# A planned four-layer graph kernel: a weight product by seven half-size products, a turned product as a 64x64 burst, and new ranks for the last pairs of groups

## The chip, the cores and the metric

The kernel runs on one core of a Trainium2 chip. That core has a matrix engine (TensorE, PE in the profile) with its own queue of weight loads (PEld), a vector engine (VectorE, DVE), a scalar engine (ScalarE, ACT), a general engine (GpSimd, POOL) and a queue that issues DMAs (SyncE, SP). Each engine works through its own list of instructions in order and waits on semaphores for the others. Products land in PSUM[...]; everything else is held in SBUF. The metric is the device time of one execution in microseconds (us).

## The reference

The input x has 128 graphs of 64 nodes with 256 features, all in fp32, and one 64 x 64 matrix `adj` is shared by all graphs. Four layers follow each other, and each ends in `x = layernorm(x + layer(x))`:

```python
# layer 0: three times a weight and the squared adjacency
h = relu(adj*adj @ (x @ W1)); h = relu(adj*adj @ (h @ W2)); y = adj*adj @ (h @ W3)
# layer 1: U holds the eigenvectors of the normalised Laplacian of adj
h = relu((U.T @ x) @ W1 + b1); y = U @ (h @ W2 + b2)
# layer 2: two graph convolutions, then LSTMs over windows of p = 1, 2, 3, 4 nodes
h = relu(adj @ (x @ Wg0 + bg0)); h = relu(adj @ (h @ Wg1 + bg1))
for p in (1, 2, 3, 4): h[:, last node of each window] = lstm_last(Wih[p-1], Whh[p-1], ..., windows of h)
# layer 3: attention over the graph
h = x @ W + b_lin; y = softmax(where(h @ h.T * adj == 0, -1e16, h @ h.T * adj)) @ h + b
```

The products of one graph with `adj`, `U` or their transposes are over 64 nodes. Two graphs fill the 128 partitions, so these products are made with 64 x 64 blocks.

## The kernel before

The 8192 rows (128 graphs x 64 nodes) are cut into 64 row tiles of 128 rows. Four row tiles are a group, and there are 16 groups.

Layer 0 and the eigenvectors come first, in an order written by hand (`layer0`, `eigen`); the change doesn't touch them. They end at about 830 us of the profile.

After that, layers 1 to 3 are not emitted in the order of the source. A planner (`Plan`) takes notes of all operations, and `Plan.run` simulates the engines with assumed costs and emits, again and again, the operation that can start first. Its rules, as far as the change and the prediction need them:

- A unit of work is a pair of groups (`unit`): layer 1 (`layer1`) and the first part of layer 2 (`to_lstm`) for each group, then the LSTMs of window 3 and 4 for both together (`long`), then the rest of layer 2 (`from_lstm`) and layer 3 (`layer3`) for each. There are eight pairs, and at most four (`UNITS`) are in flight. A new one begins when one has ended. So the list of pairs that are still to begin (`todo`) is empty once the fourth pair has ended.
- Of the operations of one engine that can start within 0.02 us of the first, the one with the lowest `rank` is taken. The rank is `op.due`, which is the group's number times `PERIOD` (17.0) less the operation's `tail`, the time of the longest chain of operations behind it in its unit. When at most `LASTS` (2) groups are left, PE prefers the group with the most operations left.
- Tiles are taken from a fixed number of slots for each kind: eight PSUM banks (`ps`), `WIDE` = 9 tiles of 1024 columns (`w`, asked for with `work()`), `NARROW` = 3 of 512 columns (`v`, asked for with `work2()`). An operation that needs a tile can't start before a slot is free.
- `products` and `run` note matmuls with 0.00167 us per column and at least 0.223 us each; a burst of 32 matmuls of 64 x 64 (`mixed`) is noted with `QUADS` = 1.17 us.

In the profile all these operations have line L162, the line of `emit`; so they are told apart by tiles and shapes.

In `layer1` (one call for each group) the rows are multiplied with the eigenvectors by a burst (`mixed(xs, u2)`), then with `bw1`, two row tiles at a time; bias and relu follow, and the result `h` is multiplied with `ut2`, a 128 x 128 matrix with the 64 x 64 eigenvector matrix twice on its diagonal and zeros elsewhere:

```python
products([(pz[:, i, :], h[:, i, :], ut2, True, True) for i in (t, t + 1)])
```

These four matmuls turn h and multiply it at the same time. ACT copies their bank to the tile `z`, which is the stationary operand of the next product.

In `to_lstm` the second weight of layer 2 (`cw1`, 256 x 256) is multiplied with the mixed rows `a` (256 x 512), half of the output at a time (`c`), in two matmuls of 512 columns into one bank each. DVE then scales, adds a bias (`scalar_tensor_tensor`) and ACT applies the relu and writes `hT`, in which nodes and graphs are exchanged.

Elsewhere the kernel already multiplies 2 x 2 blocks with seven products of blocks in place of eight (Winograd's form of Strassen's method): in layer 0 (`seven` there is a local function of the layer-0 part) and in the LSTM gates (`fast`, with sums of weights from `add_weights`). In these forms the first product stays in its PSUM bank and later ones are added to it; the bank is read several times on the way, so the products of one such chain alternate with the reads.

Of the kernel before, what the change touches and what calls it, by code (L numbers as in the profile page):

```python
# [11 lines left out]
F32 = mybir.dt.float32  # L12
AF = mybir.ActivationFunctionType
ALU = mybir.AluOpType
# [89 lines left out]
class Plan:  # L104
# [59 lines left out]
    def run(self, units, ways):  # L164
# [4 lines left out]
        def rank(op):  # L169
            if op.engine == "PE" and not todo and len(left) <= LASTS:  # L170
                return -left[op.group]
            return op.due

        def candidates(guard):
            oldest = min([u for u in going if u] or [0])
# [581 lines left out]
EPS = 1e-5  # L757
UNITS = 4
ENDING = (14, 15)
WIDE = 9  # L760
NARROW = 3
GATES = 6
ATT = 2
CELLS = 2
OUTS = 2
LASTS = 2
PERIOD = 17.0
FARS = 8

RING = 4  # L770
# [59 lines left out]
def kernel(  # L830
# [138 lines left out]
    def run(out, pairs):  # L969
        for i, (lhsT, rhs) in enumerate(pairs):  # L970
            mm(out, lhsT, rhs, i == 0, i == len(pairs) - 1)
# [85 lines left out]
    def seven(n, product, c11, c12, c21, c22, last):  # L1057

        def view(b):
            return b[:, :2 * n].rearrange("p (i n) -> p i n", i=2)  # L1060

        def add(dst, b):
            VL.tensor_add(dst, dst, b)
            if last is relu:
                relu(dst, dst)

        ch = view(bank("ch"))
        product(ch, 1, True)
        step(lambda: S.copy(c11, ch))
        yield  # L1070
        b2 = view(bank())
        product(b2, 2, True)
        step(lambda: add(c11, b2))
        yield
        product(ch, 6, False)
        step(lambda: S.copy(c12, ch))  # L1076
        yield
        b5 = view(bank("b5"))
        product(b5, 5, True)
        step(lambda: S.copy(c22, b5))  # L1080
        yield
        product(ch, 7, False)
        step(lambda: add(c22, ch))
        yield
        product(b5, 3, False)
        step(lambda: add(c12, b5))
        yield
        product(ch, 4, False)
        step(lambda: last(c21, ch))
        yield  # L1090
# [164 lines left out]
    def add_weights(p, ready):  # L1255
        ways[p] = []
        names = "igo" if p == 1 else "ifgo"
        for k, w in enumerate((wih[p - 1], whh[p - 1])):
            if w is None:
                continue  # L1260
            nq = len(names)
            s = wb.tile([P, 3, nq, P], F32, name=f"sums{p}{k}")
            if p == 4:
                spare[0] = lambda s=s: s[:, 0, 0:2, :].rearrange("p q n -> p (q n)")
            s, w = plan.tile("sums", [P, 3, nq, P], s), plan.tile("sums", [P, 2, nq * 2 * P], w)
            a11, a12, a21, a22 = whole = quarters(w)
            S1, S2, S4 = (s[:, j] for j in range(3))
            V.tensor_add(S1, a21, a22, ready=ready)
            V.tensor_sub(S2, S1, a11, ready=ready)
            V.tensor_sub(S4, a12, S2, ready=ready)  # L1270
            V.tensor_sub(a21, a11, a21, ready=ready)
            raw = [{q: x[:, i] for i, q in enumerate(names)} for x in whole]
            sums = [{q: s[:, j, i] for i, q in enumerate(names)} for j in range(3)]
            ways[p].append([raw[0], raw[1], raw[3], *sums[:2], raw[2], sums[2]])

    def products(calls, also=(), **kw):

        size = lambda x: x.at.size if isinstance(x, Part) else int(np.prod(x.shape[1:]))
        cost = sum(max(0.001673 * size(c[2]) + 0.003, 0.223) for c in calls)
        plan.note("PE", [("matmul", (o, l, r), {"start": a, "stop": z, **kw}) for o, l, r, a, z in calls], cost,  # L1280
                  also=also)
# [11 lines left out]
    def work2():  # L1293
        return plan.tile("v", [P, 512])

    def ps4(shape=(P, 512)):
        return plan.tile("ps", shape)

    def as3(t, a):
        return t.rearrange("p (a b) -> p a b", a=a)  # L1300

    def relu(dst, src):
        S.activation(dst, src, AF.Relu)

    def mixed(src, rhs):

        dst = as3(work(), 2)
        to = dst.rearrange("p c (t h n) -> p h c t n", h=2, n=N)
        ps = [ps4((P, 2, 4, N)) for _ in range(2)]
        plan.note("PE", [("matmul", (ps[h][m, c, t, :], src[hs, t, f], rhs[hs, hs]), {"start": True, "stop": True})  # L1310
                         for t in range(4) for c in range(2) for m, f, h, hs in quads(c)], QUADS)
        V.tensor_copy(to[:, 0], ps[0])
        S.copy(to[:, 1], ps[1])
        return dst
# [22 lines left out]
    def layer1(xs):  # L1337
        a = mixed(xs, u2)
        for t in range(0, 4, 2):
            V.tensor_add(xs[:, t:t + 2, :], xs[:, t:t + 2, :], ub2.unsqueeze(1).to_broadcast([P, 2, D]))  # L1340
        h = as3(work2(), 4)
        z = work2()
        pz = ps4((P, 4, P))
        for t in range(0, 4, 2):
            p = ps4((P, 2, P))
            for j in range(2):
                run(p[:, j, :], [(a[:, k, (t + j) * P:(t + j + 1) * P], bw1[:, k, :]) for k in range(2)])
            V.tensor_add(h[:, t:t + 2, :], p, wide["b_b1"].unsqueeze(1).to_broadcast([P, 2, P]))
            relu(h[:, t:t + 2, :], h[:, t:t + 2, :])
            products([(pz[:, i, :], h[:, i, :], ut2, True, True) for i in (t, t + 1)])  # L1350
        S.copy(as3(z, 4), pz)
        for t in range(0, 4, 2):
            p = ps4((P, 2, D))
            for j in range(2):
                run(p[:, j, :], [(z[:, (t + j) * P:(t + j + 1) * P], bw2)])
            V.tensor_add(xs[:, t:t + 2, :], p, xs[:, t:t + 2, :])
            norm(xs[:, t:t + 2, :], False, twice=True)

    def to_lstm(xs, there):
        a = mixed(xs, adH2)  # L1360
        Q.dma_start(there, xs, cost=0.35)
        g1 = as3(work(), 4)
        for t in range(0, 4, 2):
            p = ps4((P, 2, D))
            for j in range(2):
                run(p[:, j, :], [(a[:, k, (t + j) * P:(t + j + 1) * P], cw0[:, k, :]) for k in range(2)])
            V.tensor_add(g1[:, t:t + 2, :], p, wide["c_b0"].unsqueeze(1).to_broadcast([P, 2, D]))
            relu(g1[:, t:t + 2, :], g1[:, t:t + 2, :])
        a = mixed(g1, adT2)
        hT = plan.tile("w", [P, 1024]).rearrange("p (k n b) -> p k n b", k=2, b=8)  # L1370
        for c in range(2):
            p = ps4((P, 4, P))
            run(p, [(cw1[:, k, c * P:(c + 1) * P], a[:, k, :]) for k in range(2)])
            h = work2()
            V.scalar_tensor_tensor(as3(h, 4), rs_row.unsqueeze(1).to_broadcast([P, 4, P]), cb1[:, c:c + 1], p,
                                   op0=ALU.mult, op1=ALU.add, cost=0.666)
            S.activation(hT[:, c, :, :].rearrange("p n b -> p b n"), as3(h, 8), AF.Relu, scale=2.0, cost=0.933)
        singles(hT)
        pairs(hT)
        return hT  # L1380
# [272 lines left out]
    def unit(groups):  # L1653

        if groups[0] == 0:
            add_weights(1, 10.0)
            add_weights(2, 30.0)
            add_weights(3, 45.0)
            add_weights(4, 60.0)
        there, hTs = [], []  # L1660
        for g in groups:
            plan.group = g + 1
            x = plan.tile("rows", [P, 4, D])
            there.append(plan.tile("rest", [P, 4, D], rest[g]))
            if g < RING:
                x.tile.real, x.tile.slot, x.tile.unit = rows_of(g), g, plan.unit
                plan.slots["rows"][g] = 1e9
                for i, op in enumerate(reversed(plan.pieces)):
                    if g == RING - 1 - i // 14:
                        half = np.arange(4 * D) // (2 * D) == i // 7 % 2  # L1670
                        x.tile.past.append((op, True, (0, P), half))
            else:
                Q.dma_start(x, there[-1], cost=0.35)
            layer1(x)
            hTs.append(to_lstm(x, there[-1]))
        plan.group = groups[0] + 1
        for p in (3, 4):
            long(hTs, p)
        late = plan.late
        for g, r, hT in zip(groups, there, hTs):  # L1680
            plan.group = g + 1
            x = plan.tile("rows", [P, 4, D])
            Q.dma_start(x, r, cost=0.35, after=late)
            from_lstm(x, hT, g)
            if g in ENDING:
                layer3(x, g, 0, 2)
                layer3(x, g, 2, 2)
            else:
                layer3(x, g, 0, 4)
# [56 lines left out]
```

## Time and profile before

| | us |
|---|---|
| three runs | 2305.53, 2307.65, 2307.74 |
| median | 2307.65 |
| the profiled execution | 2305.56 |
| its span, first to last instruction | 2303.8 |
| first of layer 1's bursts (`ps<-u,X`) | 832.8 |
| last product with the second weight of layer 2 (`ps<-w,cw`) | 2122.4 |
| last store of the fourth pair of groups, and of the seventh | 1882.0, 2227.3 |
| last store of all | 2301.2 |

PE is the engine that hardly rests. The busy time of each engine in four windows of the planned part, in us:

| window | PE | DVE | ACT |
|---|---|---|---|
| 1000 to 1050 | 50.0 | 26.7 | 25.7 |
| 1450 to 1500 | 47.8 | 43.8 | 30.4 |
| 2100 to 2150 | 48.9 | 45.2 | 31.6 |
| 2250 to 2300 | 34.2 | 27.4 | 25.1 |

How to read it: each matmul's modelled end overlaps the start of the next, so the sum of their durations is more than the engine's time; the distance from one start to the next is what a matmul costs in a full queue. A fp32 matmul is two records. In a timeline the columns are start, length, engine, line, operation, output and inputs, shapes and count; the bracket at the end of a line tells how long the engine had been idle and what it waited for.

### The profile page before, as it was taken

The numbers are of one execution on the slowest core, as the hardware profiler recorded it, in microseconds if no ns is written. First come the engines' busy times: TensorE is split into PE (matmuls) and PEld (weight loads), VectorE is DVE, ScalarE is ACT, GpSimd is POOL, SyncE is SP. The second block draws the span as 40 slices with busy tenths as digits, with TensorE's granted clock in tenths as the row PEclk, the third lists the DMA queues.
The fourth block names the chain that finished last, engine by engine and source line by source line (L and its number), as shares of the span: only waits on it lengthen the run. The fifth ranks groups of instructions, "written<-read, shape, count | busy, mean of one in ns | idle before, by whom it ended". The sixth has DMA issues, their size and how long they took to land.

```text
span 2303.8 us, 51099 instructions
## 1 busy us (share of the span) xinstructions
PE 2250.2 (98%) x20132; PEld 1985.7 (86%) x20132; DVE 1730.2 (75%) x5704; ACT 1196.0 (52%) x2892; POOL 137.0 (6%) x315
## 2 busy tenths in 40 slices
PE   8999999999999989999999999999999999999996
PEld 6788888878888778999989999899899899998895
DVE  5887877777888878666857967867866876878764
ACT  3444444443444336655556655555555655655654
POOL 0000000000000010000100100100000000000001
PEclk9999999999999999999999999999999999999998
DMA  7000000000000040000201211221211211312300
GB/s 242 11 11 11 10 11 11 19 11 11 11 10 2 1 161 20 19 1 27 85 22 57 75 56 40 78 72 40 77 56 49 76 65 31 104 58 93 99 19 19
DMA packets 80113, 107.87 MB, mean 47 GB/s; under 512 B 23296, under 2 KB 64256, under 8 KB 79872
## 3 DMA queue, kind: packets, MB, share of 16 engines
q1 hardware_dynamic: 79520, 104.32, 14.1%
q8 instruction: 158, 2.59, 0.5%
q14 instruction: 83, 0.68, 0.1%
q10 hardware_dynamic: 352, 0.28, 0.0%
HBM read 57.64 MB, written 45.09 MB: 45 GB/s over the span
## 4 chain that ended last, share of the span: by engine, by line
PE 86%; DVE 9%; ACT 1%; DMA 1%; issue 1%; POOL 1%; SPq 1%; DVEq 0%; ACTq 0%; POOLq 0%
PE ps L162 53%; PE ch L965 14%; PE ps L965 9%; PE b L965 6%; PE ps L1030 2%; DVE w L162 1%; DVE X L162 1%; DVE gates L162 1%; DVE st L162 1%; POOL rs L162 1%; DMA w<-far 1%; ACT gates L162 1%; PE pa L312 1%; SPq L162 1%; DVE D L52 1%
## 5 line engine op out<-in xcount | busy, mean ns | idle before, releaser
L162 PE MATMUL ps<-w,wih 128*128 128x128 f32 (+2 forms) x2944 | 573.0, 298 | 5.1 <-DVE gates L162 4.2
L162 PEld LDWEIGHTS ps<-w,wih 128*128 128x128 f32 x2944 | 454.3, 191 | 40.0 <-issue 13.5
L162 PE MATMUL ps<-w,sums 128*128 128x128 f32 (+2 forms) x3104 | 476.8, 294 | 5.7 <-DVE w L162 5.1
L162 PEld LDWEIGHTS ps<-w,sums 128*128 128x128 f32 x3104 | 419.9, 191 | 23.4 <-DVE w L162 6.4
L162 ACT ACTIVATE gates<-gates,cbi 128x256 f32<-128x256 f32 (+4 forms) x736 | 314.5, 479 | 189.0 <-DVE gates L162 186.0
L162 DVE TENSOR_TENSOR gates<-gates,ps 128x512 f32<-128x512 f32 (+4 forms) x408 | 235.9, 583 | 191.6 <-PE ps L162 182.4
L162 ACT COPY gates<-ps 128x512 f32<-128x512 f32 (+4 forms) x408 | 205.0, 507 | 238.1 <-PE ps L162 232.7
L162 PE MATMUL ps<-hs,whh 128*128 128x128 f32 (+1 forms) x896 | 182.2, 285 | 2.3 <-DVE hs L162 2.3
L162 PE MATMUL ps<-w,whh 128*128 128x128 f32 (+1 forms) x896 | 181.1, 284 | 0.0
L162 PEld LDWEIGHTS ps<-hs,whh 128*128 128x128 f32 x896 | 140.6, 193 | 2.5 <-DVE hs L162 2.5
L162 ACT ACTIVATE gates<-ps,cbi 128x128 f32<-128x128 f32 (+2 forms) x368 | 119.3, 385 | 42.2 <-PE ps L162 41.0
L162 PEld LDWEIGHTS ps<-w,whh 128*128 128x128 f32 x896 | 139.7, 191 | 0.0
L974 ACT ACTIVATE h<-h 128x512 f32<-128x512 f32 x96 | 60.5, 630 | 150.2 <-DVE h L52 150.2
L965 PE MATMUL ch<-m,tw 128*128 128x256 f32 x512 | 124.9, 382 | 3.0 <-ACT h L1076 1.7
L965 PE MATMUL b<-ss,aw 128*128 128x256 f32 x512 | 121.9, 379 | 0.0
L965 PE MATMUL ps<-aw,m 128*128 128x512 f32 x256 | 116.2, 606 | 1.2 <-ACT m L1036 1.2
L965 PEld LDWEIGHTS ch<-m,tw 128*128 128x128 f32 x512 | 94.7, 190 | 19.1 <-DVE h L52 3.7
L965 PEld LDWEIGHTS b<-ss,aw 128*128 128x128 f32 x512 | 96.8, 190 | 12.9
L162 POOL TENSOR_SCALAR rs<-mv 128x2 f32<-128x2 f32 x96 | 25.3, 272 | 1353.1 <-DVE mv L162 1351.7
L965 PEld LDWEIGHTS ps<-aw,m 128*128 128x128 f32 x256 | 48.3, 194 | 55.5 <-issue 51.5
L162 PE MATMUL ps<-hs,sums 128*128 128x128 f32 (+1 forms) x448 | 90.6, 284 | 0.0
L1036 ACT COPY m<-ps 128x512 f32<-128x512 f32 x96 | 51.2, 587 | 75.5 <-PE ps L1030 75.0
(360 smaller groups left out, 4077.4 us busy)
## 6 DMA issues: line engine op xcount, KB each, us to landing
far<-w SPq DMA_DIRECT2D x42, 512.0 KB, 2.7
w<-far SPq DMA_DIRECT2D x168, 128.0 KB, 3.2
X<-rest SPq DMA_DIRECT2D x24, 512.0 KB, 3.4
out_dram<-X SPq DMA_DIRECT2D x64, 128.0 KB, 1.7
rest<-XA SPq DMA_DIRECT2D x12, 512.0 KB, 2.6
rest<-X SPq DMA_DIRECT2D x12, 512.0 KB, 2.7
XA<-in_x_dram SPq DMA_DIRECT2D x22, 256.0 KB, 6.0
aw<-in_a_w_dram SPq DMA_DIRECT2D x3, 1024.0 KB, 10.2
```

Of the source, the lines that this page charges most:

```text
L52: return getattr(self.engine, name)(out, *args, **kw)
L162: getattr(e, name)(*[real(x) for x in args], **{k: real(v) for k, v in kw.items()})
L312: PE.matmul(out, lhsT, rhs, start=True, stop=True)
L965: PE.matmul(out, lhsT, rhs, start=start, stop=stop, **kw)
L974: S.activation(dst, src, AF.Relu)
L1030: PE.matmul(p[h][m, k, t, :], src[hs, t, f], sqT2[hs, hs], start=True, stop=True)
L1036: S.copy(to[:, h, c:c + 2], p[h])
```

## The change

Six edits, all outside layer 0:

1. In `to_lstm` the product with `cw1` is made of seven products of 128 x 128 weight blocks with 256 columns of `a`, in place of eight in two banks. DVE makes the sums of blocks of `a` (`sums_moving`) and adds the products up (`take`, `add`); the sums of weight blocks are made once (`sums_of`).
2. In `layer1` the product with `ut2` is made of 16 matmuls of 64 x 64 after all of `h` is there; its result lies in two banks, of which DVE copies one and ACT the other.
3. Once no pair is left to begin, the rank is the group's number times `LATE` (9.0) less the tail.
4. `WIDE` is 10 and `NARROW` 5.
5. The space kept for DMA descriptors is set to 1024 bytes.
6. `sums_of("cw1", ...)` is called at the start of the first pair.

```diff
@@ Plan.run
-            return op.due
+            return op.due if todo else op.group * LATE - op.tail
@@ constants
-WIDE = 9
-NARROW = 3
+WIDE = 10
+NARROW = 5
+LATE = 9.0
@@ new functions
+    def sums_of(key, w, stationary, ready):
+        s = plan.tile("sums", [P, 3, P], wb.tile([P, 3, P], F32, name=f"sums_{key}"))
+        (w00, w01), (w10, w11) = two_by_two(plan.tile("sums", [P, 2, D], w))
+        t1, t2, t4 = (s[:, i] for i in range(3))
+        if stationary:
+            V.tensor_add(t1, w01, w11, ready=ready)
+            V.tensor_sub(t2, t1, w00, ready=ready)
+            V.tensor_sub(t4, w10, t2, ready=ready)
+            V.tensor_sub(w01, w00, w01, ready=ready)
+            sevens[key] = [None, w00, w10, t4, w11, t1, t2, w01]
...
+    def sums_moving(b, spare):
+        (b00, b01), (b10, b11) = b
+        t1, t2 = spare
+        V.tensor_sub(t1, b01, b00)
+        V.tensor_sub(t2, b11, t1)
+        V.tensor_sub(b01, b11, b01)
+        return [None, b00, b10, b11, b10, t1, t2, b01], lambda: V.tensor_sub(b10, b10, t2)
...
+    def seven(product, late, take, add):
+        chain, bank2, bank5 = (ps4((P, 2, P)) for _ in range(3))
+
+        def give(bank, i, new, also=()):
+            products(product(bank, i, new), also, skip_group_check=True)
+
+        give(chain, 1, True, (bank2,))
+        take(0, 0, chain)
+        give(bank2, 2, True)
+        add(0, 0, bank2)
+        late()
+        give(chain, 6, False)
+        take(0, 1, chain)
+        give(bank5, 5, True)
+        take(1, 1, bank5)
+        give(chain, 7, False)
+        add(1, 1, chain)
+        give(bank5, 3, False)
+        add(0, 1, bank5)
+        give(chain, 4, False)
+        take(1, 0, chain)
@@ layer1
-        pz = ps4((P, 4, P))
...
-            products([(pz[:, i, :], h[:, i, :], ut2, True, True) for i in (t, t + 1)])
-        S.copy(as3(z, 4), pz)
+        pz = [ps4((P, 4, N)) for _ in range(2)]
+        plan.note("PE", [("matmul", (pz[b][m, i, :], h[bs, i, m], ut2[bs, bs]), {"start": True, "stop": True})
+                         for i in range(4) for m, _, b, bs in quads(0)], QUADS / 4 + 0.2)
+        to = z.rearrange("p (t h n) -> p h t n", h=2, n=N)
+        V.tensor_copy(to[:, 0], pz[0])
+        S.copy(to[:, 1], pz[1])
@@ to_lstm
-        for c in range(2):
-            p = ps4((P, 4, P))
-            run(p, [(cw1[:, k, c * P:(c + 1) * P], a[:, k, :]) for k in range(2)])
-            h = work2()
-            V.scalar_tensor_tensor(as3(h, 4), rs_row.unsqueeze(1).to_broadcast([P, 4, P]), cb1[:, c:c + 1], p,
-                                   op0=ALU.mult, op1=ALU.add, cost=0.666)
-            S.activation(hT[:, c, :, :].rearrange("p n b -> p b n"), as3(h, 8), AF.Relu, scale=2.0, cost=0.933)
+        b = [[a[:, k, w * D:(w + 1) * D] for w in range(2)] for k in range(2)]
+        T = as3(work2(), 2)
+        moving, late = sums_moving(b, [T[:, i, :] for i in range(2)])
+        hs = [as3(work2(), 2) for _ in range(2)]
+
+        def product(bank, i, new):
+            return [(bank.rearrange("p a n -> p (a n)"), sevens["cw1"][i], moving[i], new, True)]
...
+        def take(c, w, p):
+            V.scalar_tensor_tensor(as3(hs[c][:, w, :], 2), rs_row.unsqueeze(1).to_broadcast([P, 2, P]), cb1[:, c:c + 1], p,
+                                   op0=ALU.mult, op1=ALU.add)
+            if (c, w) == (1, 0):
+                relu_out(1)
+
+        def add(c, w, p):
+            to = as3(hs[c][:, w, :], 2)
+            V.tensor_add(to, to, p)
+            if (c, w) == (0, 1):
+                relu_out(0)
+
+        seven(product, late, take, add)
@@ unit
+            sums_of("cw1", cw1, True, 8.0)
@@ kernel
-    nc = bacc.Bacc("TRN2", target_bir_lowering=False, num_devices=1)
+    nc = bacc.Bacc("TRN2", target_bir_lowering=False, num_devices=1, dynamic_dma_scratch_size=1024)
```

`relu_out(c)` is the relu of before, on half c of the output. A second new function, `sums_held`, isn't called.

More of the change, by code (lines that the diff above doesn't have):

```diff
@@ L1303, in relu, with two_by_two, sums_held @@
         S.activation(dst, src, AF.Relu)
+    def two_by_two(w):
+        return [[w[:, k, j * P:(j + 1) * P] for j in range(2)] for k in range(2)]
+    sevens = {}
+    def sums_of(key, w, stationary, ready):
[8 more added lines that the diff above has]
+            sevens[key] = [None, w00, w10, t4, w11, t1, t2, w01]
+        else:
+            V.tensor_sub(t1, w01, w00, ready=ready)
+            V.tensor_sub(t2, w11, t1, ready=ready)
+            V.tensor_sub(t4, w10, t2, ready=ready)
+            V.tensor_sub(w01, w11, w01, ready=ready)
+            sevens[key] = [None, w00, w10, w11, t4, t1, t2, w01]
+    def sums_moving(b, spare):
[5 more added lines that the diff above has]
+        return [None, b00, b10, b11, b10, t1, t2, b01], lambda: V.tensor_sub(b10, b10, t2)
+    def sums_held(a, spare):
+        (a11, a21), (a12, a22) = a
+        t1, t2 = spare
+        V.tensor_add(t1, a21, a22)
+        V.tensor_sub(t2, t1, a11)
+        V.tensor_sub(a21, a11, a21)
+        return [None, a11, a12, a12, a22, t1, t2, a21], lambda: V.tensor_sub(a12, a12, t2)
+    def seven(product, late, take, add):
[17 more added lines that the diff above has]
+        take(1, 0, chain)
     def mixed(src, rhs):
@@ L1370, in to_lstm, with relu_out @@
         hT = plan.tile("w", [P, 1024]).rearrange("p (k n b) -> p k n b", k=2, b=8)
-        for c in range(2):
-            p = ps4((P, 4, P))
-            run(p, [(cw1[:, k, c * P:(c + 1) * P], a[:, k, :]) for k in range(2)])
-            h = work2()
-            V.scalar_tensor_tensor(as3(h, 4), rs_row.unsqueeze(1).to_broadcast([P, 4, P]), cb1[:, c:c + 1], p,
-                                   op0=ALU.mult, op1=ALU.add, cost=0.666)
-            S.activation(hT[:, c, :, :].rearrange("p n b -> p b n"), as3(h, 8), AF.Relu, scale=2.0, cost=0.933)
+        b = [[a[:, k, w * D:(w + 1) * D] for w in range(2)] for k in range(2)]
[4 more added lines that the diff above has]
+            return [(bank.rearrange("p a n -> p (a n)"), sevens["cw1"][i], moving[i], new, True)]
+        def relu_out(c):
+            S.activation(hT[:, c, :, :].rearrange("p n b -> p b n"), hs[c].rearrange("p w (a n) -> p (w a) n", n=N),
+                         AF.Relu, scale=2.0, cost=0.933)
+        def take(c, w, p):
[9 more added lines that the diff above has]
+        seven(product, late, take, add)
         singles(hT)
```

## The prediction

> **What bounds the kernel now.** I read the page's busy times first, then the waits of TensorE (PE) in two stretches, then its timeline at the instructions that the change touches, then the last 100 us.
>
> ```profile
> PE 2250.2 (98%) x20132; PEld 1985.7 (86%) x20132; DVE 1730.2 (75%) x5704; ACT 1196.0 (52%) x2892; POOL 137.0 (6%) x315
> ...
> q1 hardware_dynamic: 79520, 104.32, 14.1%
> ```
>
> PE is busy throughout; VectorE (DVE) has a quarter free. The two stretches of waits, 900 to 2150 us and then 2150 to the end:
>
> ```profile
> PE ps L162 <- DVE w L162: 5.5, 4, 1.9
> PE ps L162 <- DVE gates L162: 1.5, 5, 0.5
> PE ps L162 <- ACT gates L162: 0.4, 1, 0.4
> ```
>
> ```profile
> PE ps L162 <- ACT X L162: 3.6, 1, 3.6
> PE ps L162 <- DVE w L162: 3.2, 1, 3.2
> PE ps L162 <- DVE gates L162: 2.7, 2, 1.8
> PE ps L162 <- DVE hs L162: 2.3, 1, 2.3
> ```
>
> In 1250 us of the planned phase PE waits 7.4 us; in the last 154 it waits 11.8 in these four rows alone. So before 2150 a microsecond of PE work removed is nearly a microsecond won, and the only place with idle time to win is the end. The busy column overstates a short matmul, because its modelled end overlaps the next; I therefore price PE work from start to start in its timeline. Each fp32 matmul leaves two records.
>
> ```profile
> 839.72 0.61 PE L162 MATMUL ps<-ut,v 128*128 128x128 f32 x4
> 840.16 0.61 PE L162 MATMUL ps<-bw,w 128*128 128x128 f32 x4
> ```
>
> ```profile
> 864.68 3.60 PE L162 MATMUL ps<-w,cw 128*128 128x512 f32 x8
> 868.11 1.89 PE L162 MATMUL ps<-cw,w 128*128 128x256 f32 x8
> 869.84 1.89 PE L162 MATMUL ps<-bw,v 128*128 128x256 f32 x8
> ```
>
> ```profile
> 1450.80 0.39 PE L162 MATMUL ps<-hs,sums 128*128 128x128 f32 x2
> 1451.12 1.16 PE L162 MATMUL ps<-u,X 64*64 64x64 f32 x64
> 1452.21 0.49 PE L162 MATMUL ps<-w,wih 128*128 128x128 f32 x2
> 1452.53 0.39 PE L162 MATMUL ps<-w,whh 128*128 128x128 f32 x2
> ```
>
> Records of 128, 256 and 512 columns cost 0.44/4 = 0.11, 1.73/8 = 0.216 and 3.43/8 = 0.429 us. A burst of 64 records of 64x64 costs 1.73 us from 1450.80 to 1452.53, less four 128-column records (0.45): 1.28 us.
>
> [...] 64 records in about 1.1 us, and an extra 0.1 us for the pair of records on either side. [...] All of this kernel's data DMAs sit in the hardware queues (line q1 above, and q10)[...].
>
> **The change, part by part.**
> *Layer 2's second weight.* Per group of 4 row tiles four matmuls of 512 columns (8 records, 3.43 us) go; seven of 256 columns (14 x 0.216 = 3.03) come. That is 0.40 us, times 16 groups 6.4 us of PE. Their weight loads, 190 ns each, stay under 216.
> On DVE, start to start, a 256-wide operation takes about 0.34 us (1452.23 to 1452.57 in its timeline) and a 512-wide one from PSUM 0.62 (1449.59 to 1450.21). Four sums, four takes and three adds come (11 x 0.34 = 3.74), two of 512 go (1.24): 2.5 us a group. The relus on ScalarE (ACT) keep their number and size. Once, four sums of the weight (0.8 us on DVE) come at the start of the phase.
> The chain of seven is serial in its bank: product 6 waits for a take to read what product 1 left, and so on. What is queued behind such a wait on PE is the other pairs' gates; four pairs in flight give PE something to do, as they do for the same seven-product form in the gates, whose waits are the 1.5 us above. I charge nothing for it; uncovered, some 1.1 us (0.43 product, 0.34 take, two hand-overs) for each of three takes, 16 times, would be 53 us at the very most.
> *Layer 1's turned product.* Per group 8 records of 128 columns (0.89 us) go; 32 records of 64x64 come. The trace of before has only bursts of 64 (and two of them back to back at 929 us, start to start 0.98 us for the first, so that a burst's own part is 0.98 and its edges 0.30). Half a burst is then 0.49 + 0.30 = 0.79: 0.10 us saved, 1.6 in all. From below, if the edges are shared with a neighbouring burst, 0.49: 6.4 in all. From above, a second set of edges where the planner breaks it up: nothing saved. I take 1.6. The planner books 0.49, so what follows on PE comes about 0.3 us later than planned; with a full PE queue this costs nothing. One copy of 512 on ACT becomes 256 on each of DVE and ACT: +0.34 us DVE, about -0.2 ACT.
> *DVE in sum.* 2.84 us x 16 = 45 us. The windows between 900 and 2150 hold 919 us of DVE in 1250 (74%), so on average it fits (77%); in the fullest window (2100 to 2150: 45.2 of 50) it doesn't fit freely. The stalls of 1.4 to 1.9 us after layer 1's first product (1458, 1639, 1818 us) come from DVE standing in order behind an operation that waits for a DMA (at 1458: 2.28 us for w<-far). More operations in that line make them neither rarer nor sure to come: I put -3 to +5 us on it, and take +1.
> *Buffers.* One more w and two more v: the seven-product form holds three v where before one was in use at a time, so most of this is consumed by the change itself. 0 to -3 us; I take -1, against the +1.
> *Ranks.* They apply once the last pair has begun, which is when the fourth pair has ended: its 32nd store to the output starts at 1882 us. From there to the end the group number counts 9 instead of 17, so later groups gain against earlier ones by the length of the work behind them. SP's and POOL's operations are ranked alike, but a row tile's load lands in 3.4 us and the reloads are mostly 8 us or more apart, so their order is covered. What it can win is PE's idle time at the end:
>
> ```profile
> 2259.44 0.39 PE L162 MATMUL ps<-w,whh 128*128 128x128 f32 x2
> 2263.00 0.30 PE L162 MATMUL ps<-ident,w 128*128 128x128 f32 x1 [3.17 <-DVE w L162]
> 2263.80 3.27 PE L162 MATMUL ps<-ident,w 128*128 128x128 f32 x15 [0.50 <-ACT w L162]
> 2270.68 2.16 PE L162 MATMUL ps<-ident,X 128*128 128x128 f32 x8 [3.60 <-ACT X L162]
> ...
> 2291.46 1.13 PE L162 MATMUL ps<-w,v 128*128 128x256 f32 x4 [0.52 <-ACT v L162]
> ```
>
> Here only the last pair is left (the pair before stored its last rows at 2227). Four holes of 1.8 to 3.6 us (2226, 2243, 2259, 2266) make 10.8, and after 2292.6 comes an 11 us coda of norms and stores that no rank removes. If the pair before comes closer to the last one, its products fill holes: at best 11 us. If its closing work comes to lie after PE's last product, it costs instead. I take -5.
>
> **The sum.** -6.4 - 1.6 + 1 - 1 - 5 = -13. The profiled execution took 2305.56 us (its span 2303.8 and 1.8 around it), within the three runs' spread below their median of 2307.65; so 2292.6 from the profile, 2294.7 from the median. I say 2294.
>
> **Rivals.**
> *Both ends gained* (20%). The holes at the end close nearly whole (-10 more than the products' 8), the mid stalls shrink by 3 and some bursts share edges (3): 2307.65 - 8 - 10 - 3 - 3 = 2284. For it: the idle time is there. Against it: the last group's own chain of norm, transpose, attention and norm stays serial.
> *DVE takes the gain* (17%). The added 45 us land in full windows; each pair of groups then brings PE one more stall like the shortest of the three at 1458, 1639 and 1818 (1.4 us x 8 = 11), on top of the forecast: 2307.65 - 13 + 11 = 2305.6, from 2300 to 2311. For it: five windows of 50 us above 43 us of DVE. Against it: the trace's waits on DVE are few and short.
> *The new ranks pile up the ends* (8%, slower). One group's closing work on DVE, by mean durations (transposes 5.3, row additions 3.3, statistics 4.5, scaling 3.2, softmax 3.0), is some 19 us. Now it lies under other pairs' products. If groups come to their end together and one such closing is pushed past PE's last product, the time is 2307.65 - 8 + 19 = 2319. It decides as soon as more than 8 us of it lands there. For it: smaller steps between groups mean exactly that earlier groups wait. Against it: DVE is only 27.4 of 50 us busy in the last 50, so half such a closing fits there.
> That the seven products do not shorten PE at all, the last way in which the change would not do what it says, I give no case of its own: the saving is counted from measured record spacing.
>
> **How the numbers follow.** Forecast 55%: 2294, own range 2288 to 2299. The others as above. Range 2281 to 2304: it leaves out the best quarter of the first rival, the upper part of the second and the third, under 20% in all. A measurement tells 0.2% (4.6 us) from no change: faster (under 2303) is 55 + 20 + a third of 17 = 81%; same, most of the rest of the 17, 10%; slower 9%.
>
> **What would show it.** For layer 2's second weight: 224 records of 256 columns (14 x 16), spaced 0.216, in place of 128 records of 512. The turned product: 32 records of 64x64, about 0.8 us from neighbour to neighbour. DVE's busy time up by 45 us or a bit more (modelled durations), PE's waits before 2150 still under 12 us, and holes of PE after 2200 of about 6 us. I am wrong if PE's waits on DVE between 900 and 2150 double, if the last PE product starts more than 15 us before the end, or if the time falls below 2281, which would mean that the ranks reach further than the holes I counted.

## The result

| | us |
|---|---|
| before, median of 4 runs | 2306.59 (2305.37 to 2307.74) |
| after, median of 4 runs | 2277.68 (2277.23 to 2282.08) |
| ratio of after to before | 0.9879, 95% interval 0.9862 to 0.9896 |
| profiled execution after, and its span | 2277.23, 2275.4 |

The kernel became 28.9 us faster. The forecast was 13 us, and its range ended at 2281: the direction was right and the size less than half.

The page of the kernel after, busy times:

```profile
PE 2233.0 (98%) x20612; PEld 1990.8 (87%) x20612; DVE 1772.5 (78%) x5868; ACT 1189.5 (52%) x2892; POOL 137.0 (6%) x315
```

To be laid beside the same line of the kernel before, shown with the prediction: DVE grew by 42 us (45 were expected). PE's modelled busy time fell by 17 us, and still reads 98%: this line doesn't tell where the time went. The timeline of PE after, at two of the seven products and at a burst of the turned product:

```profile
1090.75 1.03 PE L162 MATMUL ps<-w,cw 128*128 128x256 f32 x4
1091.62 0.38 PE L162 MATMUL ps<-w,wih 128*128 128x128 f32 x2
...
1394.95 0.39 PE L162 MATMUL ps<-w,whh 128*128 128x128 f32 x2
1395.27 0.69 PE L162 MATMUL ps<-ut,v 64*64 64x64 f32 x32
1395.89 0.49 PE L162 MATMUL ps<-w,wih 128*128 128x128 f32 x2
1396.22 0.39 PE L162 MATMUL ps<-w,whh 128*128 128x128 f32 x2
```

Four records of 256 columns take 0.87 us, as priced. The burst takes 1.27 us from 1394.95 to 1396.22, less four records of 128 columns (0.45): 0.82, where 0.79 was estimated.

The same three windows of the two kernels (columns: length, busy us of PE, PEld, DVE, ACT and POOL with counts, granted clock, DMA share, GB/s), before and then after:

```profile
1300.00:1868.00 568.00, 561.63 (x5127) 516.05 (x5126) 419.03 (x1137) 322.49 (x766) 43.10 (x82) 1.00 0.21 62
1868.00:2150.00 282.00, 280.85 (x2479) 256.12 (x2478) 217.56 (x595) 165.67 (x399) 20.68 (x42) 1.00 0.22 70
2150.00:2304.00 154.00, 128.98 (x1002) 118.76 (x1000) 93.79 (x285) 79.61 (x197) 13.85 (x40) 0.94 0.14 42
```

```profile
1300.00:1868.00 568.00, 567.88 (x5425) 532.67 (x5424) 443.48 (x1228) 332.22 (x797) 43.93 (x84) 1.00 0.19 61
1868.00:2150.00 282.00, 282.00 (x2572) 263.93 (x2571) 209.47 (x567) 167.41 (x405) 12.90 (x28) 1.00 0.16 53
2150.00:2304.00 154.00, 106.69 (x846) 94.67 (x844) 96.61 (x305) 64.84 (x158) 21.02 (x53) 0.96 0.25 76
```

From 1300 to 2150 us PE has practically no idle time left: 567.88 of 568 and 282.00 of 282. In the first window DVE does 24 us more than before while PE waits 6 us less. The waits of PE after 2150, in the kernel after:

```profile
PE ps L162 <- DVE w L162: 3.1, 1, 3.1
PE ps L162 <- ACT att L162: 2.4, 1, 2.4
PE ps L162 <- ACT X L162: 2.1, 2, 1.5
PE ps L162 <- DMA w<-far: 1.8, 1, 1.8
PE ps L162 <- ACT v L162: 1.3, 1, 1.3
```

And its end, to be laid beside the end shown with the prediction:

```profile
2232.05 0.39 PE L162 MATMUL ps<-w,whh 128*128 128x128 f32 x2
2235.53 0.33 PE L162 MATMUL ps<-ident,w 128*128 128x128 f32 x1 [3.09 <-DVE w L162]
2236.41 1.48 PE L162 MATMUL ps<-ident,w 128*128 128x128 f32 x7 [0.56 <-ACT w L162]
2237.68 3.15 PE L162 MATMUL ps<-w,att 128*128 128x256 f32 x8
...
2266.80 1.41 PE L162 MATMUL ps<-w,v 128*128 128x256 f32 x4 [1.35 <-ACT v L162]
```

The first hole, where the last gates are over, is still there (3.09 after 3.17), but then products of another group (`w,att`) follow before the transposes of the last. From the start of PE's last product to the end, in what follows called the coda, it is 7.9 us, not 11.6.

To see all of it I added up the start-to-start distances of PE's records from the first of layer 1's bursts to the last product. A record counts as work with its spacing in a full queue (0.1115, 0.1425, 0.216, 0.429 us for 128, 168, 256, 512 columns; bursts and 64-column products as they are). What exceeds that, up to double, is half clock where the trace's clock record says that PE was granted half its clock; otherwise it is a wait if PE was idle for over 0.1 us before the next record.

| us of the span | before | after | difference | the prediction's term |
|---|---|---|---|---|
| start of layer 1's first burst | 832.8 | 834.2 | +1.3 | none |
| work | 1404.8 | 1395.6 | -9.2 | -8 |
| waits and half clock to 900 | 3.9 | 2.5 | -1.4 | none |
| waits and half clock, 900 to 2150 | 10.6 | 0.3 | -10.3 | +1 - 1 |
| waits and half clock from 2150 | 19.7 | 14.1 | -5.6 | -5, the coda with it |
| small gaps | 20.3 | 21.0 | +0.7 | none |
| coda | 11.6 | 7.9 | -3.7 | |
| sum (rows are rounded) | 2303.8 | 2275.4 | -28.4 | -13 |

Two rows carry the surprise: the middle, which gained 10.3, and the end, which gained 9.3 with its coda.

The row of work depends on where short pauses go. The bursts "as they are" contain pauses of over 0.1 us, 2.8 us before and 4.3 after; counted as waits, they make the difference in work nearly -11 and that of the waits to 900 about nothing. The small gaps hold the edges that a burst leaves on the records beside it (0.32 and 0.33 us for the two records of 128 columns on either side of the burst above, 0.22 in a full queue); work and small gaps together are -8.5. So PE's own work shrank by some 8.5 to 11 us, and it isn't known better than that.

### The profile page after: what moved, and what is told of

Read it like the earlier page. It is cut to its first block, busy times and chain, and to the rows that moved or that the text cites. A ratio compares the mean times of both kernels' runs of the same rounds, so it can differ in the third digit from the quotient of the medians.

```text
span 2275.4 us, 52244 instructions
## 1 busy us (share of the span) xinstructions
PE 2233.0 (98%) x20612; PEld 1990.8 (87%) x20612; DVE 1772.5 (78%) x5868; ACT 1189.5 (52%) x2892; POOL 137.0 (6%) x315
## 3 DMA queue, kind: packets, MB, share of 16 engines
q1 hardware_dynamic: 79520, 104.32, 14.1%
## 4 chain that ended last, share of the span: by engine, by line
PE 91%; DVE 6%; issue 1%; ACT 1%; DMA 1%; POOL 0%; SPq 0%; ACTq 0%; DVEq 0%; POOLq 0%
PE ps L162 58%; PE ch L966 14%; PE ps L966 10%; PE b L966 7%; PE ps L1031 2%; PE pa L312 1%; DVE w L162 1%; DVE D L52 1%; DVE tw L52 1%; DVE X L162 1%; DVE gates L162 0%; DVE st L162 0%; DVE v L162 0%; ACT gates L162 0%; DVE h L52 0%
```

## The experiments

Theory after the result: PE's work pays as counted; the added slots removed the middle's stalls; the ranks made the end shorter. Rivals: the ranks alone made most of it; or the seven products broke up the stalls; or it is chance of a reordered plan. Times are medians; "before" is what the kernel before took beside the same runs.

### One edit taken out of the changed kernel

```diff
# o_due
-            return op.due if todo else op.group * LATE - op.tail
+            return op.due
# o_buf
-WIDE = 10
-NARROW = 5
+WIDE = 9
+NARROW = 3
# o_turn: products([(pz[:, i, :], h[:, i, :], ut2, True, True) for i in (t, t + 1)]) and one copy, as before
# o_cw1: run(p, [(cw1[:, k, c * P:(c + 1) * P], a[:, k, :]) for k in range(2)]), as before, without sums_of
```

> The changed kernel with the old rank (due) to the end. If the ranks win what the traces show at the end (coda 3.7 us shorter, half-clock time of the last 150 us 6.8 us less, waits 1 us more), taking them away costs about 9 us: 2286 to 2289, with nothing changed before 1868 us. Rival, the ranks carry most of the 16 us that the sum missed: 2293 or more. Rival, the ranks do nothing and the end moved with the rest of the schedule: within 2 us of 2278.

> The changed kernel with 9 wide and 3 narrow slots. Theory: the added slots removed the three stalls of 1.4 to 1.9 us between 1300 and 1868 and their half-clock stretch (9 us together): 2287, with waits of PE in that stretch back at 5 us or more. Rival, the stalls went with the new instruction order and the slots are consumed by the seven products: within 3 us of 2278. Rival, three narrow slots throttle the seven-product form, which holds three: above 2295.

> The changed kernel with the turned product made of four 128-column matmuls again. By the traces a burst of 32 costs 0.62 us plus its edges of 0.2, against 0.89: 1.2 us in sum, so 2279. Rival, the shorter hold of its PSUM banks or the split copy loosens the schedule: 2283 or more. Rival, the burst costs more than it saves: below 2277.

> The changed kernel with layer 2's second weight in four matmuls of 512 columns again. PE gets 6.4 us more and DVE 40 us less. Theory, PE's work alone decides: 2284. Rival, the seven products are what broke the stalls between 1300 and 1868: 2293. Rival, DVE's relief pays it back: within 2 us of 2278.

| | us | before | ratio, interval | its cost against 2277.7 |
|---|---|---|---|---|
| o_due | 2291.17 | 2307.04 | 0.9934 (0.9919 to 0.9949) | +13.5 |
| o_buf | 2350.42 | 2307.04 | 1.0194 (1.0177 to 1.0211) | +72.7 |
| o_turn | 2282.97 | 2307.04 | 0.9896 (0.9882 to 0.9911) | +5.3 |
| o_cw1 | 2285.22 | 2307.04 | 0.9907 (0.9893 to 0.9922) | +7.5 |

o_due: the ranks are worth 13 us here, between my first case (2286 to 2289) and the second (2293). The fourth pair ends at 1867.5 (1868.6 in the changed kernel), so nothing changes before. From there on the sum shows 6.8 us more of waits, 2.8 more of half clock and a coda of 12.0 in place of 7.9.

o_cw1: near "PE's work alone decides" (2284). Its waits between 900 and 2150 are 2.7 us, none of them over 0.7, so with the slots added the seven products are not needed to be rid of the stalls. o_turn came at the edge of its second case (2283), not at 2279. Its waits there are 1.4; work and small gaps cost it 1.1 us, near the 1.2 priced, and 4.4 us more of half clock account for most of the rest. That part is not the burst's own.

o_buf is the largest effect of all, and the third case that I had written: three narrow slots throttle the seven-product form, which holds three at once. The edit takes the wide slot away too, but the trace points to the narrow ones: it shows a chain of seven standing open. Its first products are made from 934.41 on and its product with a sum of `a` at 943.29 (PE); its first `take`, which has to write a narrow tile, comes at 1091.06 (DVE), 148 us after the first product, and the rest of the chain follows within 10 us. A free narrow tile is all that a `take` can lack once its product is there:

```profile
934.41 0.60 PE L162 MATMUL ps<-w,cw 128*128 128x256 f32 x2
943.29 0.60 PE L162 MATMUL ps<-v,sums_cw 128*128 128x256 f32 x2
1091.06 0.48 DVE L162 SCALAR_TENSOR_TENSOR v<-rs_row,cb,ps 128x256 f32<-128x256 f32 x1 [1.50 <-DMA att<-v]
1091.60 1.22 PE L162 MATMUL ps<-v,sums_cw 128*128 128x256 f32 x2 [4.92 <-DVE v L162]
```

In between PE runs out of other work:

```profile
1044.72 0.39 PE L162 MATMUL ps<-w,whh 128*128 128x128 f32 x2
1073.03 3.36 PE L162 MATMUL ps<-w,dw 128*128 128x512 f32 x4 [27.92 <-DMA w<-far]
```

PE stands still for 28 us, waiting for one group's rows to be written to DRAM and read back (a crossing: `far<-w`, then four `w<-far`). Which tiles held the narrow slots in that time was not followed. Between 1300 and 1868 this kernel has no wait of PE over 0.5 us (3.2 us in all). So with the products changed, the slots were not needed to remove the three stalls.

### One edit put into the kernel before

```diff
# p_rank
-            return op.due
+            return op.due if todo else op.group * LATE - op.tail
# p_buf: WIDE = 10, NARROW = 5, dynamic_dma_scratch_size=1024
# p_buf_rank: both
# p_scr: dynamic_dma_scratch_size=1024
# q_rank_w: the rank, WIDE = 10, the descriptor space
# q_rank_v: the rank, NARROW = 5, the descriptor space
```

> The kernel before with the new rank alone. Taking the rank out of the changed kernel cost 12 to 13 us, at the end (waits, half-clock time, coda). Theory, the rank works by itself: about 2295, with the three stalls of 1.4 to 1.9 us between 1300 and 1868 us still there and the coda at 8 us in place of 11.6. Rival, it needs the added slots to let the later pairs start: 2302 or more.

> The kernel before with 10 wide and 5 narrow slots and the smaller descriptor space, the products and the rank as before. Theory, slots remove the three stalls between 1300 and 1868 (9 us with the half-clock stretch): 2298. Rival, the slots serve the seven products only, and any other edit shifts the coincidence away: 2305 or more with the stalls in place.

> Slots and rank together on the kernel before, no product changed. If the parts add up, the products' own PE work of 9 us is all that is left to the changed kernel: 2286 to 2287. Rival, the products bring more than their PE work: above 2290.

> The kernel before with the smaller descriptor space alone: [...] within 1 us of the kernel before. Rival, DMAs slow down for want of descriptors: above 2309.

> The kernel before with the new rank, the smaller descriptor space and 10 wide slots; narrow slots stay at 3. The rank alone gave nothing, with both kinds of slots 17.5 us. Theory, wide slots are what the rank and the three stalls need, since the tiles that cross through DRAM and the rows of the waiting groups are wide: 2288 to 2291. Rival, the narrow ones: 2302 or more.

> The counterpart: new rank, smaller descriptor space, 5 narrow slots, wide slots stay at 9. Theory: 2300 or more, with the three stalls between 1300 and 1868 us in place. Rival, narrow slots suffice: 2288 to 2291. If each kind brings half, both runs lie near 2297.

| | us | before | ratio, interval | fourth pair's last store | from it to the span's end |
|---|---|---|---|---|---|
| p_scr | 2305.88 | 2305.96 | 0.9999 (0.9990 to 1.0008) | | |
| p_rank | 2305.86 | 2305.96 | 0.9999 (0.9991 to 1.0008) | 1883.0 | 421.4 |
| q_rank_v | 2305.60 | 2306.50 | 0.9996 (0.9988 to 1.0005) | 1881.7 | 420.3 |
| p_buf | 2299.56 | 2305.96 | 0.9972 (0.9962 to 0.9982) | 1877.2 | 420.7 |
| p_buf_rank | 2288.43 | 2305.96 | 0.9924 (0.9909 to 0.9939) | 1876.1 | 410.8 |
| q_rank_w | 2287.96 | 2306.50 | 0.9920 (0.9904 to 0.9937) | 1875.2 | 410.8 |
| before | 2306.59 | | | 1882.0 | 421.8 |
| after | 2277.68 | 2306.59 | 0.9879 (0.9862 to 0.9896) | 1868.6 | 406.8 |

The last two columns separate the middle from the end, since the ranks act from the fourth pair's end on. The slots by themselves bring 6.4 us, most of it before that store (4.8 of the 5.9 us by which the two profiles differ; waits and half clock from 900 to 2150 fall from 10.6 to 4.1); the ranks by themselves bring nothing; together they bring 17.5, with 10 to 11 of them at the end. Beside the ranks the one wide slot does what all the slots do, and the two narrow ones do nothing for these products. The smaller descriptor space alone changed nothing (p_scr, 0.9999); before that run it was not shown. I had expected p_rank at 2295; the rival, that it needs the slots, holds. p_buf_rank fell between its two cases. What is left from it to the changed kernel is 10.8 us, against 8.5 to 11 of work.

Why does a wide slot remove the stalls? In the kernel before, the stall at 1458 looks like this, DVE's line and then PE's:

```profile
1458.72 0.69 DVE L162 TENSOR_TENSOR X<-w,X 128x512 f32<-128x512 f32 x1 [2.28 <-DMA w<-far]
```

```profile
1460.59 1.12 PE L162 MATMUL ps<-w,sums 128*128 128x168 f32 x6 [1.91 <-DVE w L162]
```

DVE waits for a transfer, and PE for a sum that stands behind it. The queue of SP around that time, first in the kernel before and then in p_buf:

```profile
1444.47 5.54 SPq L162 DMA_DIRECT2D far<-w  x3
1450.11 7.56 SPq L162 DMA_DIRECT2D w<-far  x12
```

```profile
1439.84 0.33 SPq L162 DMA_DIRECT2D far<-w  x1
1442.97 1.74 SPq L162 DMA_DIRECT2D w<-far  x4
1444.76 3.15 SPq L162 DMA_DIRECT2D far<-w  x2
1448.42 3.88 SPq L162 DMA_DIRECT2D w<-far  x8
```

In the kernel before three crossings go out at once, first all three writes and then all twelve reads, which land between 3.9 and 6.1 us after their issue, where the plan books 3.0. With a tenth wide slot one crossing goes 4.6 us earlier, its four reads come before the other two writes, and the twelve land after 2.6 to 3.8. The other two stalls stand behind the same three writes and twelve reads, from 1625 and 1805, with reads of up to 5.8 and 5.6 us. At one more place the kernel before has three crossings close together, but in the order of p_buf:

```profile
1967.67 0.33 SPq L162 DMA_DIRECT2D far<-w  x1
1970.97 1.75 SPq L162 DMA_DIRECT2D w<-far  x4
1972.76 0.90 SPq L162 DMA_DIRECT2D far<-w  x2
1976.57 4.75 SPq L162 DMA_DIRECT2D w<-far  x8
```

There no read took over 4.8 us, and PE didn't wait. Among all runs, only p_scr, p_rank and q_rank_v also have three writes in a row between 1300 and 1868, and only they also have the stalls. If that reading is right, a plan that expects the DMAs to be late should also remove the stalls, with nine slots:

```diff
# r_lag, and s_lag with 4.0 on the changed kernel
-    LAG = {"PE": 0.205, "DVE": 0.13, "ACT": 0.14, "POOL": 0.0, "SP": 3.0}
+    LAG = {"PE": 0.205, "DVE": 0.13, "ACT": 0.14, "POOL": 0.0, "SP": 4.5}
```

> The kernel before with one figure of the planner changed: it expects a DMA to land 4.5 us after its issue, in place of 3.0; slots, rank and products as before. Theory: the three stalls come from twelve transfers of three crossings queued together, which land up to 6 us after issue, later than planned; a planner that expects it puts other work there, and the kernel gains the stalls' 9 us: 2297 to 2300. Rival, the ninth wide slot was short and the estimate is no matter: 2304 or more, stalls still there.

r_lag took 2305.01 beside 2305.57 (1.0002, 0.9993 to 1.0011). The three stalls are gone (PE's longest wait between 1300 and 1868 is 0.6 us), at most two writes go out in a row there, no read takes over 4.9 us, and the fourth pair ends at 1867.9, 14 us earlier than in the kernel before. That agrees with the reading of the stalls but doesn't prove it: p_scr, p_rank and q_rank_v keep PE's order of the kernel before up to the fourth pair's end, and every run that changes it earlier has lost the stalls. That any new order would have done as much is not excluded. And the expected gain did not come, the time is the same: from that store to the end it is 434.9 us, 13 more than before. The same matmuls are only put in another order, so what one stretch does less of is left for the next; a milestone such as the fourth pair's end tells of order as well as of time, and only the sum of waits tells of loss. That sum fell from 10.6 to 6.5 us in the middle, while the row of work is 2.2 higher, 1.6 of it pauses at bursts, and the start 1.3 later. So the plain removal of three stalls was worth some 3 to 4 us here, and scattered small losses hid it.

### Is the ranks' gain an optimum or one lucky order?

The edit is the value of LATE in the changed kernel; o_due is the old rank, with 17.

> The changed kernel with LATE 12 in place of 9, between the new rank and the old one (17, which gave 2291). If the gain follows the step between groups: 2281 to 2284, with the last pairs' ends further apart than in the changed kernel. Rival, a threshold: as the changed kernel, within 2 us of 2278.

> The changed kernel with LATE 6. The rival of the prediction, that the closing work of several groups piles up behind PE's last product, should come in here if anywhere: 2285 or more, with a coda above 10 us or waits of PE on DVE. Otherwise the ends come closer and it stays within 3 us of 2278.

> The changed kernel with LATE 8. LATE 6, 9, 12 and 17 gave 2291, 2278, 2291 and 2291. Theory, 9 hits one favourable order of the last two groups (they end 6 us apart and the coda is 8 us in place of 12): a neighbour may miss it, 2283 to 2292, with a coda near 12. Rival, a smooth optimum: 2278 to 2281.

> The changed kernel with LATE 10. Theory, one favourable order: 2283 to 2292 with a coda near 12, unless the last two groups end staggered as in the changed kernel. Rival, a smooth optimum: 2278 to 2281.

| LATE | us | ratio, interval | waits and half clock from 1868 | last product to the end | last stores of groups 15th and 16th to end |
|---|---|---|---|---|---|
| 6 | 2290.80 | 0.9932 (0.9917 to 0.9946) | 20.5 | 11.6 | 2281.6, 2285.6 |
| 8 | 2280.07 | 0.9889 (0.9873 to 0.9905) | 16.5 | 8.3 | 2267.6, 2274.7 |
| 9 | 2277.68 | 0.9879 (0.9862 to 0.9896) | 14.1 | 7.9 | 2266.5, 2272.9 |
| 10 | 2286.15 | 0.9915 (0.9899 to 0.9931) | 19.3 | 11.6 | 2279.3, 2282.7 |
| 12 | 2290.67 | 0.9930 (0.9915 to 0.9945) | 23.4 | 12.0 | 2282.7, 2286.1 |
| 17, old rank | 2291.17 | 0.9934 (0.9919 to 0.9949) | 23.7 | 12.0 | 2281.4, 2284.9 |

It is not a smooth function of the step: 10 loses 8.5 us against 9, and 6 and 12 nearly all of the ranks' gain. So most of the 13 us hangs on one favourable order, and as far as the prediction goes that order is luck. LATE 12 came in neither of its cases, and LATE 8 in its rival's. The two that win have their last two groups end 6 to 7 us apart and a coda near 8; the others 3 to 4 us apart and a coda near 12. When the two groups end together, the last norms of both stand behind each other on POOL after PE's last product; in the kernel after only one pair of row tiles is left there. POOL after PE's last product, the long step of the norms, in the kernel before (three pairs of row tiles) and then after (one):

```profile
2295.37 0.71 POOL L162 TENSOR_TENSOR rs<-rs,half 128x2 f32<-128x2 f32 x1
2297.08 1.36 POOL L162 TENSOR_TENSOR rs<-rs,half 128x2 f32<-128x2 f32 x2
```

```profile
2270.47 0.71 POOL L162 TENSOR_TENSOR rs<-rs,half 128x2 f32<-128x2 f32 x1
```

The coda is not everything: p_rank also has 8.0 us, and no gain, because its waits and half-clock time from 2150 are 21.9. Too much of the ranks (LATE 6) costs what the old rank costs, through waits of PE on DVE (8.8 us in two), which is the mild form of the piling-up that I had as a rival.

### Attempts at a better version

```diff
# r_quads
-                         for i in range(4) for m, _, b, bs in quads(0)], QUADS / 4 + 0.2)
+                         for i in range(4) for m, _, b, bs in quads(0)], QUADS / 2 + 0.2)
# s_wide11
-WIDE = 10
+WIDE = 11
```

> The changed kernel with the burst of the turned product booked at 0.785 us in the plan, near the 0.82 that it takes, in place of 0.49. A truer plan could win the few stalls at its start (850 to 890 us, 2.5 us): 2275 to 2277. Rival, any change of the plan reorders the end and loses the favourable order: 2283 or more.

> The changed kernel with 11 wide slots in place of 10. The tenth brought 17 us together with the rank, on the kernel before. If wide slots are still short: 2268 to 2275. Rival, the tenth was the one that was missing: no stall is left before 2150 us for the eleventh to remove, and the plan of the end is only reordered: 2277 to 2290.

> The changed kernel with the plan's DMA landing at 4.0 us in place of 3.0. On the kernel before, 4.5 us removed the three stalls and gave the gain back at the end. Here the only wait of PE for a DMA is the one of 1.8 us at 2183: 2274 to 2277 if the end keeps its order. Rival, the end is reordered and loses it: 2281 or more.

r_quads took 2281.18 (0.9893, 0.9875 to 0.9911), s_wide11 2280.94 (0.9883, 0.9867 to 0.9900), s_lag 2283.59 (0.9895, 0.9880 to 0.9910). None beats the changed kernel, and the intervals of all three overlap its own (0.9862 to 0.9896), so that the 3 to 6 us between the medians are not clear of noise. Their work, 1394.3 to 1397.1 us, is that of the changed kernel; they lose 2.7 to 3.6 us more to half clock and up to 2.5 to waits. My reading is that a truer burst or DMA time in the plan, or an eleventh slot, reorders the end, and that the end as it is was already favourable.

## Why the prediction was wrong

**PE's work: right.** "6.4 us of PE" for the second weight: o_cw1 costs 7.5, 6.7 of it work when pauses at bursts count as waits. "1.6 in all" for the turned product: the burst took 0.82 where 0.79 was taken, so 1.2; o_turn costs 5.3, of which most is half-clock time. In sum -8.5 to -11 in the trace against -8. DVE's +45 was +42 and found room: waits of PE on DVE between 900 and 2150 fell to nothing instead of doubling. The rival that DVE takes the gain falls.

**The middle: the failed term.** "0 to -3 us; I take -1, against the +1" was some 10 us short. I had the stall's cause in hand (DVE in order behind a wait for w<-far) and called it neither rarer nor sure to come; I did not look at the DMA queue behind it, where three crossings sit in one lump. I also priced the slots as one thing, "most of this is consumed by the change itself". That is true of the narrow ones (without any of the added slots: +72.7) and false of the wide one, with which alone (q_rank_w) the kernel before loses its stalls. Which edit removed the stalls in the changed kernel isn't unique: a wide slot alone does it, a later DMA time in the plan does it, and o_buf, without the slots but with the products, does not have them either. I take them for a coincidence of the plan that any of these edits dissolves; so the 10 us were in the trace to be seen, but that the change would win them was not to be derived from it.

**The ranks: mis-sized, and with a wrong bound.** "At best 11 us" and "an 11 us coda of norms and stores that no rank removes". The ranks were worth 13 us in the changed kernel (o_due): 6.8 of waits, more than the 5 that I took, 4 us in that very coda, and 2.8 of half-clock time, which I had left out although the page's last slice (8 tenths) and the clock column of the windows (0.94 from 2150) show it. Holes of PE after 2200 were to be about 6 us and are 9.5.

**Adding up: wrong in principle here.** The sum treats five edits as independent. The ranks alone give 0, beside the added slots 11, with the products as well 13. The slots alone give 6.4, and the change without them is 43 us slower than the kernel before. Of the rivals, "both ends gained" (2284) comes nearest in size; I gave it 20%. Its mechanism holds in part: the mid stalls shrank, but by 10 us and not by 3, and the holes at the end did not close nearly whole; waits after 2150 fell by 2.8 us, and the rest of the end's 9.3 is half clock and coda. The sign "if the time falls below 2281" came, but "that the ranks reach further than the holes I counted" explains the smaller part of what was missing: 4.3 us at the end, against 10 in the middle.

**Open.** What the nine wide slots keep from happening at the end, so that the ranks do nothing there, is not shown: p_rank has one stall of 3.9 us at 2199, on DVE, that p_buf_rank has not, but I didn't follow it to a slot. Whether the stalls went because the crossings were parted, or whether any other order would have been rid of them, is open too. That LATE 9 is favourable with this plan is shown; why 10 is not, beyond the order of the last two groups, is not.

## What to carry to other kernels

When a planner or a greedy scheduler writes the order, an edit is worth its own work, which can be counted to two or three microseconds here from start-to-start spacing, plus a reordering, which can't: take the size of the reordering from the waits of the whole stretch that it can touch, as a range, and test edits together and one out, not only one by one. Add up work, waits, half clock and coda separately, and don't read a gain from an intermediate milestone. Where an engine waits behind a transfer, look at what else is in the DMA queue at that moment, and at how many buffers let those transfers begin at different times.

## What the runs showed of the hardware

Half clock was not in my price. PE's timeline before, after the wait of 2.27 us that ended at 2245.65:

```profile
2246.65 0.39 PE L162 MATMUL ps<-hs,whh 128*128 128x128 f32 x2
2246.87 0.52 PE L162 MATMUL ps<-w,wih 128*128 128x128 f32 x2
...
2247.61 0.64 PE L162 MATMUL ps<-w,wih 128*128 128x128 f32 x2
2248.04 0.63 PE L162 MATMUL ps<-hs,whh 128*128 128x128 f32 x2
```

From about 2247.0 two records take 0.43 us in place of 0.22, for 3.4 us, in which the granted clock is 0.50. In the clock records of all twenty profiles every half-clock stretch that the end doesn't cut off is about a multiple of 3.4 us (40 of 3.4 us, 43 of 6.8, four longer). After 900 us, and not counting the last 8 us of PE's work, all 32 waits of PE of 3 us or more, 17 of them shorter than 3.4 us, had a half-clock stretch over them or within 5 us after, 6 of 24 between 1.7 and 3 us had one, and 5 of 28 between 1 and 1.7. (The kernels share most of their plans, so these waits are not independent of each other.) The wait of 1.91 us at 1458 was followed by one in the kernel before and by none in p_scr, whose wait is 1.91 us too: twelve records of 128 columns (`ps<-bw,w`), which start 0.96 us after its end, take 2.21 us in the one and 1.33 in the other. From 0.43 us against 0.22 I estimate that 3.4 us of half clock lose up to 1.7 us of work. So this stall cost 1.9 us in one profile and by that estimate up to 3.6 in the other, and its length doesn't tell which; those of 3 us or more were all met by a stretch (32 of 32). From layer 1's first burst to PE's last product half clock took some 8 us before, 1.7 after.
